# Moving part of a convolution's opening to GpSimd in a residual chain kernel

## The chip, the cores and the metric

The kernel runs on one core of one Trainium2 chip. The metric is the device time of one execution in microseconds; the median of three runs of the kernel before is 2248.76 us (2246.2 to 2252.79). The engines are named as the profile names them: PE is TensorE (matmuls), PEld its weight loads, DVE is VectorE, ACT is ScalarE, POOL is GpSimd and SP is SyncE, which issues most DMAs.

## The reference

The input is x of shape [32, 64, 1024] (batch, channel or row, position), and four lists of 32 integers. Four residual steps follow one another:

```python
x = x + conv(x, log_dt, C, log_A_real, A_imag, D, length)   # long convolution
x = x + einsum('bsi,boi->bso', x, w1[ids1])                  # adapter 1
x = x + einsum('bij,bkj->bik', x, w2[ids2])                  # adapter 2
x = x + lora_mlp(x, ids3)                                    # gated MLP with low-rank parts
```

Only the first matters for this change. Its kernel is a sum over 64 complex states for each of the 64 channels:

```python
dtA = (-exp(log_A_real) + 1j * A_imag) * exp(log_dt)[:, None]
Ct  = (C[..., 0] + 1j * C[..., 1]) * (exp(dtA) - 1) / A
K   = 2 * einsum('hn,hnl->hl', Ct, exp(dtA[:, :, None] * arange(1024))).real
y   = causal_convolution(x, K) + x * D[:, None]
```

and y is set to zero from each sequence's length on.

## The kernel before, in words

The convolution runs on chunks of 128 positions. For each pair of channels (32 pairs, held as 128 partitions = 2 channels x 64 states) the kernel needs powers of z = exp(dtA). It forms z to 37 chosen exponents (0, 32, 64, 96; 1 to 32; 128) as a magnitude (an exponential of the real part times the exponent) times a cosine and a sine of the phase times the exponent. From these few tables all 129 powers of a pair are made as products of two of them.

The pairs go through in groups of four, eight groups in all, and each group in two units of two pairs. The tables are made in two parts: part 0 holds the 8 pairs of groups 0 and 1, part 1 the 24 pairs of groups 2 to 7. A table row of part 0 has 8 x 37 = 296 columns, one of part 1 has 24 x 37 = 888.

For a unit, `products` (on ACT, 16 small activations, L1575) or `products_now` (on DVE, four tensor_tensor operations) write the products `m`; two DVE sums, kept in `adds`, turn them into the powers `zs`, and a POOL copy writes their first column (L1557). `powers_turned` transposes the powers on PE (L1624) and ACT copies them to `e` (L1637). `inputs` multiplies the input blocks by them on PE (L1655), and ACT copies the result to the states `xg` (L1663). `kernels` makes the convolution's first 128 taps (PE L1675, ACT L1692) and SP writes them to a scratch in DRAM, `kps`, whose rows begin with 128 zeros that POOL's queue wrote before; `load_taps` reads them back as a shifted matrix `hk`. `direct` applies the taps within a chunk (L1754). `scan` is the recurrence that carries the states from chunk to chunk: six steps of three dependent DVE operations. `carried` adds the states' part on PE (L1770), and `taken` masks the result and adds it to x on DVE.

The order of the work is written out by hand for DVE, ACT, POOL, SP and PE: each engine runs its instructions in the order in which the program emits them. `run(steps, events)` takes the steps of a recurrence one by one and inserts each event after the given number of steps; `spread` gives consecutive numbers. `opening` fills the pipeline before the first regular `period`: its units 0 to 2 come ahead of the first recurrence, its fourth unit (group 1, unit 1) between that recurrence's steps. The arguments of part 1 (`raised(1, ...)`, `fraction`) are made on DVE between the units, its exponential on ACT at L1877, its cosine and sine (`turned`) at L1338, L1339 and L1402, the products of magnitude and phase (`sizes`), the tables (`tables(1)`, `sz`) and the five small tables (`small_tables(1)`: `taps`, `turn`) between the recurrence's later steps. Helpers record most operations, so DVE's lines are mostly L1310 (`tt`), L1315 and L1317 (`ts`) and L1321 (`stt`), and the tiles tell them apart. Weights of the adapters are prefetched on SP's queue all along (`fetch`), into buffers that come free as the convolution ends.

The argument of part 1's exponential lies in `work[0]`, which is also the scratch of `tables`. The tile `opened` holds part 0's magnitude and, behind it, the zero row; the recurrence's scratch `t` takes the same buffer afterwards.

Of the kernel before, what the change touches and what calls it, by code (L numbers as in the profile page):

```python
# [19 lines left out]
P = 128  # L20
# [1215 lines left out]
def convolution(tc, cst, consts, xt, xf, ssm, eye, lens, x0, cd, ps_tile, fetch, places, rows_now, first):  # L1236
# [12 lines left out]
    with ExitStack() as ctx:  # L1249
# [53 lines left out]
        def small():  # L1303
            return space(NP)

        def col(i):
            return cst[:, i : i + 1]

        def tt(o, a, b, op):
            nc.vector.tensor_tensor(o, a, b, op)  # L1310
            return o

        def ts(o, a, c0, op0, c1=None, op1=None):
            if op1 is None:
                nc.vector.tensor_scalar(o, a, c0, None, op0)  # L1315
            else:
                nc.vector.tensor_scalar(o, a, c0, c1, op0, op1)  # L1317
            return o
# [12 lines left out]
        def fraction(v, k):  # L1331

            ts(k, v, MAGIC, ALU.add)
            stt(v, k, MAGIC, v, ALU.subtract, ALU.subtract)

        def cosine(o, r, k, scale=1.0):

            nc.scalar.activation(k, r, AF.Abs)  # L1338
            nc.scalar.activation(o, k, AF.Sin, scale=-scale, bias=col(CO_HALF))  # L1339

        def flipped(v, d):

# [27 lines left out]
        def by_part(pool, name, shape):  # L1370
# [5 lines left out]
        zts, szs = by_part(s1, "zt", [NL]), by_part(s1, "sz", [NA])  # L1376
        turns, tapss = by_part(g0, "turn", [2]), by_part(s1, "taps", [2, NA])
        rhos = [
            v[:, : (q1 - q0) * NL].rearrange("p (q l) -> p q l", l=NL)
            for v, (q0, q1) in zip((opened, work[0]), parts)  # L1380
        ]

        def of(tiles, q0, q1):
            i = int(q0 >= N0)
            return tiles[i][:, :, q0 - parts[i][0] : q1 - parts[i][0]]

        def raised(i, o, v):

            q0, q1 = parts[i]
            tt(  # L1390
                o,
                v[:, q0:q1].unsqueeze(2).to_broadcast([P, q1 - q0, NL]),
                cst[:, CO_LVAL : CO_LVAL + NL].unsqueeze(1).to_broadcast([P, q1 - q0, NL]),
                ALU.mult,
            )

        def turned(i, between=None):
            k, r = zts[i][:, 0], zts[i][:, 1]
            cosine(k, r, k, TURN)
            if between:  # L1400
                between()
            nc.scalar.activation(r, r, AF.Sin, scale=-TURN)  # L1402

        def sized(i):
# [3 lines left out]
        def tables(i):  # L1408


            q0, q1 = parts[i]
            n = q1 - q0
            t = work[0][:, : 4 * n * NA].rearrange("p (s j q a) -> p s j q a", s=2, j=2, a=NA)
            z = zts[i][:, :, :, :NA]
            s = [
                v[:, q0:q1].unsqueeze(1).unsqueeze(3).to_broadcast([P, 2, n, NA])
                for v in (s_re, s_im)
            ]
            tt(t[:, 0], z, s[0], ALU.mult)
            tt(t[:, 1], flipped(z, 1), s[1], ALU.mult)  # L1420
            for j, op in enumerate((ALU.subtract, ALU.add)):
                tt(szs[i][:, j], t[:, 0, j], t[:, 1, j], op)

        def small_tables(i):
            n = parts[i][1] - parts[i][0]

            def taps(j):
                side = cst[:, CO_SIDE + 2 * j : CO_SIDE + 2 * j + 2]
                tt(
                    tapss[i][:, j],  # L1430
                    szs[i][:, j].unsqueeze(2).to_broadcast([P, n, 2, NA]),
                    side.unsqueeze(1).unsqueeze(3).to_broadcast([P, n, 2, NA]),
                    ALU.mult,
                )

            def turn():
                z = [zts[i][:, j, :, NL - 1] for j in range(2)]
                nc.vector.tensor_copy(turns[i][:, 0], z[0].unsqueeze(2).to_broadcast([P, n, 2]))
                nc.vector.tensor_copy(turns[i][:, 1, :, 1], z[1])
                ts(turns[i][:, 1, :, 0], z[1], -1.0, ALU.mult)  # L1440

            return (lambda: taps(0)), (lambda: taps(1)), turn

# [17 lines left out]
        gp(pi, cre, aim, ALU.mult)  # L1461
        gp(v, cim, ea, ALU.mult)
        gp(pi, pi, v, ALU.add)
        t, em, ep, yh, u, sh, ch, w = (small() for _ in range(8))
        nc.scalar.activation(t, x, AF.Tanh, scale=0.5)
        nc.scalar.activation(rhos[0], rhos[0], AF.Exp)
        turns_off(y, u, (C1, C2, C3))
        ts(yh, y, 0.5, ALU.mult)
        ts(r, y, 1.0 / TWO_PI, ALU.mult)
        raised(0, zts[0][:, 1], r)  # L1470
        fraction(zts[0][:, 1], zts[0][:, 0])
        nc.scalar.activation(sh, yh, AF.Sin)
        cosine(ch, yh, w)
        turned(0)
        ts(em, t, -1.0, ALU.mult, 1.0, ALU.add)
        nc.vector.reciprocal(em, em)
        stt(em, t, 2.0, em, ALU.mult, ALU.mult)
# [35 lines left out]
        tt(rm, rm, m0, ALU.add)  # L1513
        stt(h4, acr, 2.0, rm, ALU.mult, ALU.add)
        nc.scalar.activation(m0, h4, AF.Sqrt)
        nc.vector.reciprocal(rm, m0)
        tt(rm, rm, h4, ALU.mult)
        tt(rm, rm, m0, ALU.add)
# [11 lines left out]
        tables(0)  # L1530

        kps = dram.tile([H, KROW], F32, tag="kp", name="kp")
        zero = opened[:H, N0 * NL : N0 * NL + P]
        nc.gpsimd.memset(zero, 0.0)
        nc.gpsimd.dma_start(kps[:, :P], zero)

        lnf = g0.tile([P, B], F32, tag="lnf", name="lnf")
        mask = g0.tile([P, NCK, KT, BC], F32, tag="mask", name="mask")
        maskf = mask.rearrange("p c k b -> p (c k b)")
        nc.gpsimd.tensor_copy(lnf, ln)  # L1540

        powers = {}

# [39 lines left out]
        def products_now(g, u, js=(0, 1), new=None):  # L1583
            m, q = new or new_powers(g, u)
            fs = []
            for j in js:
                z = of(zts, q + j, q + j + 1)[:, :, 0]
                s = of(szs, q + j, q + j + 1)[:, :, 0]
                for c in range(2):

                    def product(j=j, c=c, z=z, s=s):
                        tt(
                            m[:, c, j],
                            z[:, :, NA : NA + LQ].unsqueeze(2).to_broadcast([P, 2, NA, LQ]),
                            s[:, c].unsqueeze(1).unsqueeze(3).to_broadcast([P, 2, NA, LQ]),
                            ALU.mult,
                        )

                    fs.append(product)
            return fs  # L1600
# [16 lines left out]
        def powers_turned(g, u):  # L1617

            i_ = first_unit[g] + u
            zs = powers[i_]  # L1620
            ps = ps_tile(f"pt{i_}").rearrange("p (j i t) -> p j i t", j=2, i=2)
            for j in range(2):
                for i in range(2):
                    nc.tensor.matmul(  # L1624
                        ps[:, j, i],
                        zs[:, i, j, :P],
                        unit,
                        start=(i == 0 and j == 0),
                        stop=True,
                        is_transpose=True,  # L1630
                        skip_group_check=True,
                    )
# [226 lines left out]
        def opening():  # L1859


            warm(WARM)
            m0 = new_powers(0, 1)
            made(products(0, 1, (0,), m0))
            now(products_now(0, 0))
            added_now(0, 0)
            powers_turned(0, 0)()
            now(products_now(0, 1, (1,), m0))
            added_now(0, 1)
            powers_turned(0, 1)()  # L1870
            raised(1, rhos[1], x)
            now(small_tables(0))
            now(products_now(1, 0))
            added_now(1, 0)
            raised(1, zts[1][:, 1], r)
            fraction(zts[1][:, 1], zts[1][:, 0])
            nc.scalar.activation(rhos[1], rhos[1], AF.Exp)  # L1877
            inputs(0, 0)
            inputs(0, 1)
            kernels(0)  # L1880
            load_taps(0)
            fetch(MID)
            powers_turned(1, 0)()
            fourth = products_now(1, 1)
            sizes = [
                lambda j=j: tt(zts[1][:, j], zts[1][:, j], rhos[1], ALU.mult) for j in range(2)
            ]

            def second():
                turned(1, powers_turned(1, 1))  # L1890
                inputs(1, 0)
                inputs(1, 1)
                kernels(1)
                direct(0, 0)
                direct(0, 1)

            def third():
                tables(1)
                for u in range(2):
                    made(products(2, u))  # L1900

            run(
                scan(0),
                [
                    *spread(1, fourth),
                    *spread(5, adds.pop((1, 1))),
                    (7, second),
                    (8, masks),
                    *spread(9, sizes),
                    (10, third),  # L1910
                    *spread(12, small_tables(1)),
                ],
            )
            load_u(2)
            load_taps(1)
# [300 lines left out]
```

## Time and profile before

| | |
|---|---|
| median of three runs | 2248.76 us |
| the profiled execution | 2251.07 us, of which the span is 2249.4 us |
| granted TensorE clock, mean | 0.998 |
| busy: PE, PEld | 2198.9 us (98%), 1803.9 us (80%) |
| busy: DVE, ACT, POOL | 1370.9 us (61%), 424.1 us (19%), 207.5 us (9%) |
| DMA | 656.35 MB, mean 292 GB/s |
| convolution | from the start to about 143 us, where the adapters' matmuls (L315) begin to follow one another |

The page gives the busy time of each engine, the chain of work that ended last, and the costliest groups. As the shares are means over stages with different limits, a change in the opening is read from the timelines of the first 50 us: each line has the start, the time of one or more equal instructions, the engine, the line of the program, what is written from what, and, in brackets, an idle time before it and what ended it. Busy spans on POOL are rough.

### The profile page before, as it was taken

To read this page: it belongs to the slowest core of one execution; us is meant where nothing else is said; L and a number is where in the kernel's file an instruction comes from. 1 tells how busy PE (TensorE), PEld (TensorE's weight loads), DVE (VectorE), ACT (ScalarE), POOL (GpSimd) and SP (SyncE) were. 2 spreads that over 40 slices of the span, in tenths; PEclk is the share of its full clock that TensorE was granted. 3 is DMA by queue.
4 is the path that set the end of the run, shared out by engine and by line. 5 is a ranking of instruction groups with operands and counts; after the bars stand their busy time and mean duration, and the time that the engine had idled before them with its cause. 6 is when DMAs were issued, how large, how long until landed. Compare 5 with 4: busy or idle time off the path is not lost.

```text
span 2249.4 us, 53713 instructions
## 1 busy us (share of the span) xinstructions
PE 2198.9 (98%) x21488; PEld 1803.9 (80%) x21488; DVE 1370.9 (61%) x2995; ACT 424.1 (19%) x1042; POOL 207.5 (9%) x328
## 2 busy tenths in 40 slices
PE   7989999999999999999999999999999999999999
PEld 5755587777687897888688887789678988899998
DVE  8961277666367767466345667466336666576575
ACT  6800121111010112121012212022002212121220
POOL 1001021111012211000000111000000010100000
PEclk9999999999999999999999999999999999999999
DMA  8799998899979658799979839799979938385581
GB/s 312 252 316 401 386 359 306 316 363 356 344 294 354 241 174 303 290 366 358 351 266 367 298 128 343 263 337 358 364 281 354 337 116 282 111 291 189 203 278 63
DMA packets 204683, 656.35 MB, mean 292 GB/s; under 512 B 24066, under 2 KB 40834, under 8 KB 203922
## 3 DMA queue, kind: packets, MB, share of 16 engines
q1 hardware_dynamic: 173122, 565.84, 69.4%
q0 software_dynamic: 23392, 76.07, 9.2%
q10 hardware_dynamic: 7920, 11.01, 1.3%
q8 instruction: 169, 2.77, 0.5%
q14 instruction: 80, 0.66, 0.1%
HBM read 585.66 MB, written 67.17 MB: 290 GB/s over the span
## 4 chain that ended last, share of the span: by engine, by line
PE 79%; DMA 10%; DVE 6%; issue 4%; POOL 1%; ACT 1%; SPq 0%; POOLq 0%; DVEq 0%; ACTq 0%
PE pq L694 29%; PE po L1104 24%; PE pa L315 13%; DMA wa<-in_w 7%; PE pf L593 6%; PE pr L342 3%; PE pe L462 2%; DVE xg L1310 1%; PE pl_d L433 1%; DMA sums<-kept 1%; DVE t L1310 1%; DMA wr_first<-in_wr 1%; DVE tmp L1310 1%; PE pr_first L342 0%; ACT m L1575 0%
## 5 line engine op out<-in xcount | busy, mean ns | idle before, releaser
L315 PE MATMUL pa<-wa,x 128*32 128x256 f32 x7680 | 441.1, 380 | 16.7 <-DMA wa<-in_w 15.5
L694 PE MATMUL pq<-xd,wa 128*128 128x128 f32 x3360 | 414.9, 275 | 0.1
L315 PEld LDWEIGHTS pa<-wa,x 128*32 128x32 f32 x7680 | 238.4, 110 | 202.5 <-DMA wa<-in_w 42.1
L694 PEld LDWEIGHTS pq<-xd,wa 128*128 128x128 f32 x3360 | 394.6, 192 | 0.5 <-DMA wa<-sums 0.3
L694 PE MATMUL pq<-xd,wb 128*128 128x128 f32 x2520 | 323.6, 276 | 0.0
L694 PEld LDWEIGHTS pq<-xd,wb 128*128 128x128 f32 x2520 | 300.5, 192 | 3.6
L325 DVE STREAM_TRANSPOSE y<-pa 128x512 f32<-128x512 f32 x64 | 45.9, 717 | 287.9 <-PE pa L315 287.9
L1104 PE MATMUL po<-act,wd 128*128 128x256 f32 x640 | 168.6, 386 | 0.0
L1104 PE MATMUL po<-actd,wd 128*128 128x256 f32 x640 | 164.2, 379 | 0.0
L1104 PE MATMUL po<-actd,s 128*128 128x256 f32 x640 | 164.2, 379 | 0.0
L488 DVE TENSOR_TENSOR s<-wd 128x256 f32<-128x256 f32 x80 | 33.8, 423 | 176.5 <-PE po L1104 176.4
L1104 PEld LDWEIGHTS po<-act,wd 128*128 128x128 f32 x640 | 117.8, 190 | 29.3 <-issue 13.9
L593 PE MATMUL pf<-xd,wf 128*128 128x256 f32 x576 | 135.5, 381 | 0.0
L1104 PEld LDWEIGHTS po<-actd,s 128*128 128x128 f32 x640 | 121.6, 190 | 16.5
L1104 PEld LDWEIGHTS po<-actd,wd 128*128 128x128 f32 x640 | 121.6, 190 | 16.5
L1136 ACT COPY uo<-po 128x256 f32<-128x256 f32 x48 | 17.9, 373 | 620.1 <-PE po L1104 603.8
L361 POOL DMA_INDIRECT bgu<-in_bgu,rows x44 | 44.6, 1013 | 963.8 <-PE pe L462 798.4
L593 PEld LDWEIGHTS pf<-xd,wf 128*128 128x128 f32 x576 | 108.7, 190 | 15.5
L593 PE MATMUL pf<-xd,s 128*128 128x256 f32 x480 | 114.4, 381 | 1.0 <-DVE up L634 0.6
L718 ACT COPY u<-pq 128x256 f32<-128x256 f32 x120 | 41.5, 346 | 370.1 <-PE pq L694 303.2
L593 PEld LDWEIGHTS pf<-xd,s 128*128 128x128 f32 x480 | 90.3, 190 | 16.6 <-DVE up L634 2.7
L723 DVE TENSOR_TENSOR u<-u,u 128x256 f32<-128x256 f32 x120 | 46.6, 388 | 73.6 <-ACT u L720 73.6
(273 smaller groups left out, 2762.4 us busy)
## 6 DMA issues: line engine op xcount, KB each, us to landing
wa<-in_w SPq DMA_DIRECT2D x480, 512.0 KB
wa<-sums SPq DMA_DIRECT2D x210, 512.0 KB
wb<-parts SPq DMA_DIRECT2D x120, 384.0 KB
wd<-in_wd SPq DMA_DIRECT2D x80, 512.0 KB
wb<-in_wq SPq DMA_DIRECT2D x90, 384.0 KB
sums<-kept POOLq DMA_DIRECT2D x30, 1024.0 KB, 7.5
wf<-in_wu SPq DMA_DIRECT2D x20, 512.0 KB
uf<-in_xf SPq DMA_DIRECT2D x16, 512.0 KB
```

What stands on the lines that cost most here:

```text
L315: nc.tensor.matmul(acc[i * S : (i + 1) * S, s * 256 : (s + 1) * 256], xs[c][:, kt, lo + s * S : lo + (s + 1) * S], wt[:, i * 256 : (i + 1) ...
L325: nc.vector.transpose(y, acc)
L342: nc.tensor.matmul(ps[:, tokens], wt[:, kt, :], xs[c][:, kt, tokens], start=(kt == 0), stop=(kt == KT - 1),)
L361: nc.gpsimd.indirect_dma_start(out=t, out_offset=None, in_=table, in_offset=bass.IndirectOffsetOnAxis(ap=at_, axis=0),)
L462: nc.tensor.matmul(ps[:, at_ * 2 * H : (at_ + 1) * 2 * H], bt[pair(j), g], tms[table][pair(j)], start=(g == 0), stop=True, skip_group_chec ...
L488: nc.vector.tensor_add(s1, a21, a22)
L593: nc.tensor.matmul(ps, ws[j][:, kt, :], xb[j][:, kt, :], start=start and kt == 0, stop=kt == KH - 1, skip_group_check=True,)
L694: nc.tensor.matmul(ps[:, to * TQ : (to + 1) * TQ], w[i][:, k, :], xb[:, j, SLOT[i], k, :], start=start and k == 0 and to == 0, stop=k == K ...
L718: nc.scalar.copy(u, pa)
L723: nc.vector.tensor_add(u, v, u)
L1104: nc.tensor.matmul(pss[j], *term, start=(s0 == m0 and i == 0 and home[j] % 2 == 0), stop=(end and i == len(terms) - 1 and not late), skip_ ...
L1310: nc.vector.tensor_tensor(o, a, b, op)
```

## The change

Six things change in the opening.

- The argument of part 1's exponential (`raised(1, rhos[1], x)`, 888 columns) goes from DVE to POOL, right after POOL's nine small products; it is written behind the first 128 columns of `work[0]`, clear of the scratch of `tables(0)`.
- The phase argument of part 1 (888 columns) goes to POOL as well, as four operations: the product, MAGIC added, MAGIC subtracted, and the difference that is left. On DVE it had been a product and two operations.
- Part 1's exponential on ACT goes from between the units to right behind the second square root.
- The zero row (memset, DMA) and the cast of the lengths go from right after those products on POOL's queue to behind the copies of the first two units.
- The fourth unit with its transposes, the magnitude (Abs), cosine and sine of part 1, the second group's inputs and kernels and the first group's direct products are emitted ahead of the first recurrence; the magnitude stands ahead of the third unit. Between the steps there remain the masks, the sizes and the tables.
- The five small tables of part 1 go to POOL, after `tables(1)`.

```diff
-            v[:, : (q1 - q0) * NL].rearrange("p (q l) -> p q l", l=NL)
-            for v, (q0, q1) in zip((opened, work[0]), parts)
+            v[:, at_ : at_ + (q1 - q0) * NL].rearrange("p (q l) -> p q l", l=NL)
+            for v, at_, (q0, q1) in zip((opened, work[0]), (0, 4 * N0 * NA), parts)
...
         gp(pi, pi, v, ALU.add)
+        raised(1, rhos[1], x, nc.gpsimd)
...
         ts(r, y, 1.0 / TWO_PI, ALU.mult)
+        k1, r1 = zts[1][:, 0], zts[1][:, 1]
+        raised(1, r1, r, nc.gpsimd)
+        nc.gpsimd.tensor_scalar(k1, r1, MAGIC, None, ALU.add)
+        nc.gpsimd.tensor_scalar(k1, k1, MAGIC, None, ALU.subtract)
+        gp(r1, k1, r1, ALU.subtract)
         raised(0, zts[0][:, 1], r)
...
         nc.scalar.activation(m0, h4, AF.Sqrt)
+        nc.scalar.activation(rhos[1], rhos[1], AF.Exp)
...
             powers_turned(0, 1)()
-            raised(1, rhos[1], x)
+            zeros()
+            second = turned(1)
+            next(second)
             now(small_tables(0))
             now(products_now(1, 0))
             added_now(1, 0)
-            raised(1, zts[1][:, 1], r)
-            fraction(zts[1][:, 1], zts[1][:, 0])
-            nc.scalar.activation(rhos[1], rhos[1], AF.Exp)
             inputs(0, 0)
             inputs(0, 1)
             kernels(0)
             load_taps(0)
             fetch(MID)
             powers_turned(1, 0)()
-            fourth = products_now(1, 1)
+            now(products_now(1, 1))
+            added_now(1, 1)
+            next(second, None)
+            powers_turned(1, 1)()
+            inputs(1, 0)
+            inputs(1, 1)
+            kernels(1)
+            direct(0, 0)
+            direct(0, 1)
...
             def third():
                 tables(1)
+                now(small_tables(1, nc.gpsimd))
                 for u in range(2):
                     made(products(2, u))
 
             run(
                 scan(0),
                 [
-                    *spread(1, fourth),
-                    *spread(5, adds.pop((1, 1))),
-                    (7, second),
-                    (8, masks),
+                    (7, masks),
                     *spread(9, sizes),
-                    (10, third),
-                    *spread(12, small_tables(1)),
+                    (11, third),
                 ],
             )
```

`turned` now yields after its magnitude, so that the cosine and the sine can be emitted later; `zeros` is a function that holds the memset, the DMA and the cast; `raised` and `small_tables` take the engine as an argument.

More of the change, by code (lines that the diff above doesn't have):

```diff
@@ L1334, in fraction, with cosine @@
             stt(v, k, MAGIC, v, ALU.subtract, ALU.subtract)
-        def cosine(o, r, k, scale=1.0):
+        def cosine(o, r, k):
             nc.scalar.activation(k, r, AF.Abs)
-            nc.scalar.activation(o, k, AF.Sin, scale=-scale, bias=col(CO_HALF))
+            nc.scalar.activation(o, k, AF.Sin, scale=-1.0, bias=col(CO_HALF))
         def flipped(v, d):
@@ L1385, in of, with raised @@
             return tiles[i][:, :, q0 - parts[i][0] : q1 - parts[i][0]]
-        def raised(i, o, v):
+        def raised(i, o, v, engine=nc.vector):
             q0, q1 = parts[i]
-            tt(
+            engine.tensor_tensor(
                 o,
@@ L1395, in raised, with turned @@
             )
-        def turned(i, between=None):
+        def turned(i):
             k, r = zts[i][:, 0], zts[i][:, 1]
-            cosine(k, r, k, TURN)
-            if between:
-                between()
+            nc.scalar.activation(k, r, AF.Abs)
+            yield
+            nc.scalar.activation(k, k, AF.Sin, scale=-TURN, bias=col(CO_HALF))
             nc.scalar.activation(r, r, AF.Sin, scale=-TURN)
@@ L1422, in tables, with small_tables @@
                 tt(szs[i][:, j], t[:, 0, j], t[:, 1, j], op)
-        def small_tables(i):
+        def small_tables(i, engine=nc.vector):
             n = parts[i][1] - parts[i][0]
@@ L1428, in taps @@
                 side = cst[:, CO_SIDE + 2 * j : CO_SIDE + 2 * j + 2]
-                tt(
+                engine.tensor_tensor(
                     tapss[i][:, j],
@@ L1437, in turn @@
                 z = [zts[i][:, j, :, NL - 1] for j in range(2)]
-                nc.vector.tensor_copy(turns[i][:, 0], z[0].unsqueeze(2).to_broadcast([P, n, 2]))
-                nc.vector.tensor_copy(turns[i][:, 1, :, 1], z[1])
-                ts(turns[i][:, 1, :, 0], z[1], -1.0, ALU.mult)
+                engine.tensor_copy(turns[i][:, 0], z[0].unsqueeze(2).to_broadcast([P, n, 2]))
+                engine.tensor_copy(turns[i][:, 1, :, 1], z[1])
+                engine.tensor_scalar(turns[i][:, 1, :, 0], z[1], -1.0, None, ALU.mult)
             return (lambda: taps(0)), (lambda: taps(1)), turn
@@ L1473, in convolution @@
         cosine(ch, yh, w)
-        turned(0)
+        for _ in turned(0):
+            pass
         ts(em, t, -1.0, ALU.mult, 1.0, ALU.add)
@@ L1532, in convolution @@
         kps = dram.tile([H, KROW], F32, tag="kp", name="kp")
-        zero = opened[:H, N0 * NL : N0 * NL + P]
-        nc.gpsimd.memset(zero, 0.0)
-        nc.gpsimd.dma_start(kps[:, :P], zero)
         lnf = g0.tile([P, B], F32, tag="lnf", name="lnf")
@@ L1539, in convolution, with zeros @@
         maskf = mask.rearrange("p c k b -> p (c k b)")
-        nc.gpsimd.tensor_copy(lnf, ln)
+        def zeros():
+            zero = opened[:H, N0 * NL : N0 * NL + P]
+            nc.gpsimd.memset(zero, 0.0)
+            nc.gpsimd.dma_start(kps[:, :P], zero)
+            nc.gpsimd.tensor_copy(lnf, ln)
         powers = {}
@@ L1887, in opening @@
             ]
[L1889 to L1895, printed above, removed]
             def third():
                 tables(1)
+                now(small_tables(1, nc.gpsimd))
                 for u in range(2):
```

## The prediction

> **What bounds the kernel now.** I read the page's busy shares first, then the chain of work that ended last in order of time, then the stretches of ten microseconds over the first 200 us, then the timelines of VectorE (DVE), ScalarE (ACT) and GpSimd (POOL) over the opening. TensorE is busy for 98% of the whole span, but the edit sits in the first 45 us, and there the stretches read like this (busy us and instruction counts of each engine, granted clock, DMA share, GB/s):
>
> ```profile
> 20.00:30.00 10.00, 6.90 (x66) 4.46 (x64) 9.76 (x26) 7.92 (x21) 1.35 (x4) 1.00 0.99 396
> 30.00:40.00 10.00, 5.71 (x28) 3.54 (x30) 9.90 (x24) 5.82 (x8) 0.00 (x0) 0.67 0.65 224
> 40.00:50.00 10.00, 9.38 (x82) 7.32 (x78) 9.35 (x25) 9.34 (x37) 1.12 (x4) 0.99 0.82 279
> 120.00:130.00 10.00, 8.50 (x66) 6.86 (x65) 9.62 (x26) 2.04 (x5) 0.00 (x0) 1.00 0.99 345
> 160.00:180.00 20.00, 17.39 (x304) 8.76 (x296) 2.81 (x4) 0.00 (x0) 8.81 (x16) 1.00 1.02 386
> ```
>
> DVE (third number) is the bound from 3 us to the end of the convolution: 9.4 to 9.9 of 10, while POOL is nearly empty. DVE's waits for others up to 143 us are 3.3 us for the first load, 1.6 us for ACT's products in three pieces, 1.0 us for TensorE and 0.4 us for a root. Does a microsecond saved here reach the end? The chain says what follows:
>
> ```profile
> 142.40 0.61 DVE x L1310
> 143.05 16.22 PE pa L315 x296
> 160.86 12.16 DMA wa<-in_w
> 173.14 12.40 DMA wa<-in_w
> ```
>
> The adapters start with DVE's last sum, and soon wait for weights. That stream keeps the DMA at 1.01 to 1.03 from 140 to 260 us, and its start is tied to the convolution: the last eight prefetches are issued at 135.53, when the direct products end (131.70 + 3.69), and the rotating loads at 143.75, when matmuls free buffers. From 30 to 140 us the DMA has slack (shares of 0.50 to 0.65 in three stretches). So I carry a shift of the convolution's end one to one to the end of the span.
>
> **What leaves DVE.** DVE's timeline (start, duration):
>
> ```profile
> 23.64 1.08 DVE L1310 TENSOR_TENSOR work<-work,cst 128x888 f32<-128x888 f32 x1
> 27.27 1.08 DVE L1310 TENSOR_TENSOR zt<-work,cst 128x888 f32<-128x888 f32 x1
> 28.38 0.62 DVE L1315 TENSOR_SCALAR zt<-zt 128x888 f32<-128x888 f32 x1
> 29.04 1.08 DVE L1321 SCALAR_TENSOR_TENSOR zt<-zt 128x888 f32<-128x888 f32 x1
> 30.04 0.69 DVE L1310 TENSOR_TENSOR t<-xg,turn 128x512 f32<-128x512 f32 x1
> 43.04 0.69 DVE L1310 TENSOR_TENSOR t<-xg,turn 128x512 f32<-128x512 f32 x1
> 43.76 0.88 DVE L1310 TENSOR_TENSOR xg<-xg,t 128x256 f32<-128x256 f32 x2
> 44.75 0.69 DVE L1310 TENSOR_TENSOR t<-xg,turn 128x512 f32<-128x512 f32 x1
> 45.85 0.42 DVE L1310 TENSOR_TENSOR zs<-m 128x256 f32<-128x256 f32 x1 [0.41 <-ACT m L1575]
> ```
>
> By start-to-start times the decay argument is worth 1.00 us (23.64 to 24.64), the phase argument with its fraction 2.77 (27.27 to 30.04), the five small tables 3 x 0.27 = 0.81: 4.58 us leave DVE. But the fourth unit (four products, two sums, 2.13 us by the third unit's 25.14 to 27.27) used to sit between the dependent steps of the first recurrence, and the tables too. A bare step takes 1.71 us (43.04 to 44.75); step two with three fillers of 0.34 took 2.28 (32.32 to 34.60), so 1.26 without them: 0.45 us of latency per bare step. Steps one, two and five become bare.
>
> The new DVE schedule, laid out from these rows: second unit done at 23.64; small tables 0.50, third unit 2.13, fourth unit 2.13: recurrence from 28.40. Two bare steps 3.42; step three with the mask 1.73; the sizes 1.00 and 1.11, step four's parts 0.60 + 0.34 + 0.45, the second part's tables 1.01; two bare steps 3.42. The next period starts at 41.5 instead of 44.75: 3.3 us earlier.
>
> **What could be late next.** ACT: the exponential with its table load (25.05 to 27.28) goes to behind the second root (16.52), where ACT idles 3.44 us before 19.96 and needs 1.28 + 0.94 = 2.22; if that cover fails, the excess falls on the eight products at 19.96. Then the magnitude ends at 26.0, the four state copies follow TensorE's products (ending 27.5) to 28.0, in time for 28.40; the table load and two sines (1.28 + 1.03 + 0.94, after the third unit's turned copy at 29.4) end at 32.7, and the sizes need them at 33.6 and 35.2. State copies of the second group then follow to about 36, the kernel row to 37, and the 16 products of the third group, gated by the tables, run from 37.5 to 41.4 (3.85 us), before the sum that waited 0.41 us at 45.85. So that wait goes too: 3.7 us in all. The zero row's memset, descriptor (0.76 us) and cast move on POOL's queue from 10.11 to about 22; the zero row shares a buffer with the recurrence's scratch, so the first step now waits for that DMA, and so does the first tap load (31.98 before). Some 5 us remain for it to land; if they don't suffice, each missing microsecond counts in full. SP's order of issues stays as it was.
>
> **What POOL costs.** No row shows an 888-column operation on POOL. Its memsets of 128 and 512 columns take 0.196 and 0.518 us: 0.84 ns a column, so 0.83 us for 888 if nothing but one stream counts; that is the lower end, 4.2 us for five. The upper end scales a 32-column row with its 0.24 us spacing by columns: 6.7 us each, 33 us. I take 0.83 for the two one-input operations and twice the stream, 1.58, for the three two-input ones: 6.4 us, POOL done near 17. I lean to the memset because most of a 32-column row is fixed cost. The Trainium skill (GPSIMD Engine Reference, Elementwise side-by-side) gives 4497 ns for 2048 fp32 columns of a two-input sum; my estimate from it is 1.95 us for 888, and the five would make some 7.5.
>
> **The shared read path**, the decisive unknown:
>
> ```profile
> 7.38 0.55 POOL L1456 TENSOR_TENSOR work<-par 128x32 f32<-128x32 f32 x1
> 7.39 0.45 DVE L1310 TENSOR_TENSOR opened<-work,cst 128x296 f32<-128x296 f32 x1
> 8.49 0.27 POOL L1459 TENSOR_TENSOR work<-par 128x32 f32<-128x32 f32 x1
> 49.52 2.40 POOL L1557 COPY zs<-sz 128x4 f32<-128x4 f32 x1 [2.10 <-PE py L1770]
> 51.79 0.68 DVE L1310 TENSOR_TENSOR tmp<-py,mask 128x512 f32<-128x512 f32 x1
> ```
>
> POOL's 32-column operation takes twice its usual time exactly when DVE reads two SBUF operands for 0.45 us. The copy of four columns, 0.19 us elsewhere, lasts 2.40 us and ends when DVE turns from such operations to one that reads PSUM and one SBUF operand (51.79). So DVE shuts POOL out. Whether a long POOL operation shuts DVE out, this trace cannot show: its POOL operations are too short. Bounds: nothing, to POOL's whole streaming, 6.4 us; a gain is excluded, as contention takes no work away. From 10.2 to 20 us DVE runs a serial chain of 32-column operations of about 0.2 us, most with two SBUF operands; POOL finds a gap after each and then streams. If exclusion works both ways, DVE gets about one operation in for each POOL operation: 6.4 - 5 x 0.2 = 5.4 us of delay. I take that end, because the only rows that show the two engines meeting show one shut out, and 0.5 us more for the small tables beside the bare steps (two of 192 columns, 0.41 each by the same slope, and three short ones). Nothing hides this; the chain feeds the first table at 19.96, and all later work.
>
> The Trainium skill (SBUF — State Buffer, Who interferes with whom) speaks against the change: a DVE instruction with two SBUF inputs and a GpSimd one that reads SBUF exclude each other, and whichever comes second "fully blocks" until the first finishes. The rows above agree for DVE first; for POOL first no run here shows it. By that rule and the other page's 7.5 us, the delay would be near 6.5; with ports that don't meet, nothing.
>
> **The sum.** -3.7 + 5.4 + 0.5 = +2.2 us. The profiled execution took 2251.07 us (span 2249.4 and 1.7 around it), 2.3 above the median of the runs shown (2248.76); on the median's scale: 2251.0.
>
> **Rivals.** (1) *No exclusion of DVE by POOL*: -3.7, 2245.1. For it: DVE's three-operand steps beside POOL between 8.2 and 8.9 us come every 0.225 us, no slower than the 0.25 us of the 64-column steps before POOL begins; against it, POOL streamed little there. (2) *POOL's queue is late* (slower): in its order the copies of the first column of the first unit stand behind the five operations, and TensorE's first transpose at 22.0 needs them; ACT's magnitude stands ahead of the state copies and needs the fifth. It decides when five operations take more than 22.0 - 10.2 = 11.8 us, 2.4 each; at 4 us each the transposes come 8.2 us late, which less 3.7 gives +4.5, and with some of the exclusion some +8: 2257. For it: the lower ends are linear guesses and three patterns broadcast; against it, the memset's slope would have to be three times off. (3) *More than it says*: TensorE's clock fell to 0.67 at 30 to 40 us after an idle 5.5 us; a kept clock would shorten the state products (5.52 us there, 3.25 at full clock) by 2.3 us. But DVE is the bound there, so this helps only if the waits for ACT's products go with it: at most the 1.2 us left of them, and with rival 1 and smaller bubbles some -7: 2242.
>
> **Chances.** Forecast 0.52 (2248 to 2254), rival 1 0.30 (2243.5 to 2247), rival 2 0.12, rival 3 0.06. The range 2243 to 2256 leaves out rival 3 and most of rival 2. About 0.3% (6.7 us) is what a measurement of this kernel can tell from no change: forecast and rival 1 lie within it, so same 0.81, slower 0.12, faster 0.07.
>
> **What would show it.** Exclusion: the first table's products start on DVE near 25.5 us instead of 19.96, with DVE operations of 1 to 2 us among the 32-column ones after 10 us. Rival 1: they start at 20 and the next period near 41.5. Rival 2: the first transpose waits for POOL. Wrong altogether: a first recurrence waiting for the zero row's DMA, or a convolution end whose shift is not met at 300 us.

## The result, and the profile after

The changed kernel takes 2251.24 us (median of 16 runs, 2248.33 to 2258.55) beside 2248.15 us of the kernel before on the same chips. The ratio is 1.0021 with a 95% interval of 1.0012 to 1.0030: some 4.7 us (2.7 to 6.7) slower, less than the 0.3% bound of the forecast. A second comparison gave 1.0017 (1.0007 to 1.0027). The profiled execution took 2250.81 us, with a span of 2249.1 us.

The stretches of the changed kernel, in the columns of before:

```profile
20.00:30.00 10.00, 3.22 (x14) 1.79 (x12) 9.10 (x37) 5.14 (x13) 3.54 (x8) 0.67 0.98 392
30.00:40.00 10.00, 8.36 (x75) 5.59 (x74) 7.89 (x20) 7.56 (x13) 0.00 (x0) 0.82 0.03 10
40.00:50.00 10.00, 7.16 (x62) 5.77 (x64) 9.62 (x20) 8.22 (x31) 3.40 (x7) 1.00 0.96 349
160.00:180.00 20.00, 17.32 (x284) 9.36 (x280) 3.41 (x5) 0.00 (x0) 7.97 (x15) 0.91 1.02 373
```

Two things are new. PE has 3.22 us of work from 20 to 30 us where it had 6.90, and its granted clock is 0.67 there and 0.82 in the next stretch (1.00 and 0.67 before). And DVE, once at 9.90 from 30 to 40 us, is busy for 7.89 us there, so idle for 2 us. From 160 us on the weights bound the kernel again. The chain shows the later start of the adapters:

```profile
144.85 0.61 DVE x L1310
145.50 13.63 PE pa L315 x248
160.19 9.74 DMA wa<-in_w
```

POOL's five argument operations, and beside them what happened to DVE (start, duration; both timelines of the changed kernel):

```profile
10.14 1.99 POOL L1390 TENSOR_TENSOR work<-work,cst 128x888 f32<-128x888 f32 x1
12.10 1.70 POOL L1390 TENSOR_TENSOR zt<-work,cst 128x888 f32<-128x888 f32 x1
13.89 2.47 POOL L1473 TENSOR_SCALAR zt<-zt 128x888 f32<-128x888 f32 x1
16.44 2.45 POOL L1474 TENSOR_SCALAR zt<-zt 128x888 f32<-128x888 f32 x1
18.97 2.07 POOL L1475 TENSOR_TENSOR zt<-zt 128x888 f32<-128x888 f32 x1
```

```profile
10.49 1.68 DVE L1317 TENSOR_SCALAR work<-work 128x32 f32<-128x32 f32 x1
12.20 0.35 DVE L1483 RECIPROCAL work<-work 128x32 f32<-128x32 f32 x1
12.59 1.25 DVE L1321 SCALAR_TENSOR_TENSOR work<-work 128x32 f32<-128x32 f32 x1
14.42 0.47 DVE L1321 SCALAR_TENSOR_TENSOR work<-work 128x32 f32<-128x32 f32 x1
16.63 0.83 DVE L1310 TENSOR_TENSOR work<-work 128x64 f32<-128x64 f32 x1
19.01 2.08 DVE L1310 TENSOR_TENSOR work<-work 128x32 f32<-128x32 f32 x1
25.30 1.43 DVE L1310 TENSOR_TENSOR m<-zt,sz 128x256 f32<-128x256 f32 x4
35.67 0.69 DVE L1310 TENSOR_TENSOR t<-xg,turn 128x512 f32<-128x512 f32 x1 [1.83 <-issue]
```

Read the two side by side. A DVE operation on 32 columns takes some 0.2 us otherwise (0.17 to 0.19 us next to these rows); here one lasts 1.68 us and ends at 12.17, just after POOL's first product does (12.13); one lasts 2.08 us and ends at 21.09, after POOL's last (21.04). The three long ones fall on POOL's three two-operand products. During POOL's one-operand operations, which last longest, DVE loses only some 0.3 and 0.6 us. The reciprocal keeps its 0.35 us. So the first table's products start at 25.30 us instead of 19.96: 5.34 us late. The last line is a new wait of 1.83 us, and PE's timeline shows where it comes from:

```profile
27.34 1.15 PE L1634 MATMUL pt<-unit,zs 128*128 128x128 f32 x4 [6.37 <-DVE zs L1310]
29.96 5.04 PE L1665 MATMUL pv<-uf,e 128*64 128x224 f32 x32
```

PE sat idle for 6.37 us, because the first powers were late, and the 32 state products behind it took 5.04 us instead of the 3.25 us of before. Here is their row in PE's timeline of before, and the last of ACT's copies of the states in the changed kernel's:

```profile
24.26 3.25 PE L1655 MATMUL pv<-uf,e 128*64 128x224 f32 x32
35.05 0.53 ACT L1673 COPY xg<-pv 128x448 f32<-128x448 f32 x1 [0.23 <-PE pv L1665]
```

The copies follow the products, and the first recurrence needs the copies: the last one ends at 35.58 us, and the recurrence starts at 35.67. The profile itself names nothing that DVE waited for here ("issue"); the experiments below do.

### The profile page after: what moved, and what is told of

Same layout as the page of the kernel before. It is cut to its first block, busy times and chain, and to the rows that moved or that the text cites. A ratio compares the mean times of both kernels' runs of the same rounds, so it can differ in the third digit from the quotient of the medians.

```text
span 2249.1 us, 53710 instructions
## 1 busy us (share of the span) xinstructions
PE 2197.9 (98%) x21488; PEld 1806.3 (80%) x21488; DVE 1372.0 (61%) x2986; ACT 424.5 (19%) x1042; POOL 220.9 (10%) x338
## 4 chain that ended last, share of the span: by engine, by line
PE 82%; DMA 9%; DVE 5%; issue 3%; POOL 0%; ACT 0%; SPq 0%; POOLq 0%; DVEq 0%; ACTq 0%
PE pq L694 29%; PE po L1104 24%; PE pa L315 14%; PE pf L593 7%; DMA wa<-in_w 5%; PE pr L342 3%; DMA wa<-sums 2%; PE pe L462 2%; DVE xg L1310 1%; PE pl_d L433 1%; DVE t L1310 1%; DVE tmp L1310 1%; DMA wr_first<-in_wr 1%; DMA sums<-kept 1%; PE pr_first L342 0%
## 5 line engine op out<-in xcount | busy, mean ns | idle before, releaser
L325 DVE STREAM_TRANSPOSE y<-pa 128x512 f32<-128x512 f32 x64 | 45.8, 716 | 283.1 <-PE pa L315 283.1
L718 ACT COPY u<-pq 128x256 f32<-128x256 f32 x120 | 41.5, 346 | 371.5 <-PE pq L694 304.9
```

Source lines behind the costliest of these rows:

```text
L325: nc.vector.transpose(y, acc)
L718: nc.scalar.copy(u, pa)
```

## The experiments

The theory was that a long GpSimd operation shuts DVE out of the path that both use, and that this, less what DVE no longer does, is the whole change. Rivals: no such exclusion, with the new order to blame; a wait for the zero row's DMA instead of a clock drop; and a gain or loss in the opening that does not reach the end. This table collects the marks (us from the span's start, from DVE's and PE's timelines); "16th sum" is the start of the 16th of the 64 adapter transposes (L325). Medians stand beside the kernel before on the same chip.

| kernel | first products | first recurrence | next period | adapters | 16th sum | median / before | ratio (95%) |
|---|---|---|---|---|---|---|---|
| before | 19.96 | 30.04 | 44.75 | 143.05 | 283.4 | | |
| before_again | 19.97 | 30.05 | 44.76 | 143.00 | 283.6 | 2249.27 / 2248.40 | 1.0006 (0.9995 to 1.0017) |
| changed | 25.30 | 35.67 | 48.87 | 145.50 | 285.5 | 2251.24 / 2248.15 | 1.0021 (1.0012 to 1.0030) |
| after_again | 25.23 | 35.83 | 49.03 | 145.62 | 286.4 | 2251.86 / 2248.40 | 1.0017 (1.0007 to 1.0027) |
| args_dve | 19.89 | 32.10 | 45.28 | 142.72 | 282.5 | 2247.72 / 2248.54 | 0.9997 (0.9986 to 1.0009) |
| args_only | 25.26 | 35.44 | 50.16 | 146.65 | 285.9 | 2250.38 / 2248.54 | 1.0009 (0.9999 to 1.0020) |
| after_warm | 25.32 | 33.78 | 46.97 | 144.40 | 285.3 | 2254.23 / 2248.54 | 1.0028 (1.0019 to 1.0037) |
| args_short | 19.90 | 28.38 | 41.57 | 139.09 | 278.6 | 2246.53 / 2248.45 | 0.9997 (0.9988 to 1.0006) |
| args_short_again | 20.00 | 28.48 | 41.67 | 138.19 | 278.5 | 2246.51 / 2248.40 | 0.9996 (0.9985 to 1.0008) |
| tables_only | 19.95 | 30.03 | 44.74 | 141.27 | 281.7 | 2247.77 / 2248.45 | 1.0000 (0.9991 to 1.0010) |
| exp_act | 19.96 | 29.05 | 43.76 | 141.91 | 281.7 | 2249.42 / 2248.45 | 1.0009 (0.9999 to 1.0019) |
| exp_act_fill | 19.90 | 28.98 | 43.70 | 140.88 | 282.7 | 2249.39 / 2248.45 | 1.0002 (0.9992 to 1.0012) |
| exp_tables | 20.01 | 29.09 | 43.80 | 141.79 | 283.2 | 2247.30 / 2248.40 | 0.9993 (0.9982 to 1.0004) |

**ports: the disputed cost by itself.** A kernel of its own, run once, in phases; most have one chain on DVE and a few operations on GpSimd:

```python
for _ in range(2):
    G.tensor_tensor(g3, gb[0], gb[1], ALU.mult)      # or tensor_scalar, or memset; 888 columns
for _ in range(24):
    V.scalar_tensor_tensor(v, v, 1.0, w[:, :32], ALU.mult, ALU.mult)   # or another kind
```

> A small kernel that leaves the whole computation out and only measures the two engines side by side: VectorE chains of 24 dependent operations of 128x32 (two SBUF operands, one operand, reciprocal, one PSUM operand) alone and beside two 888-column GpSimd operations, and 20 independent 128x256 products beside the same. Mutual exclusion: the two-operand chain alone takes about 24 x 0.22 = 5.4 us; beside two products on GpSimd of some 1.9 us each it takes 3 to 4 us more, with single VectorE operations stretched to 1.5 us and more; the reciprocal chain and the chain with a PSUM operand are not stretched; memsets on GpSimd cost the chain nothing. Beside the long independent VectorE products it is GpSimd that is held, until they end (some 6.8 us). Exclusion of GpSimd by VectorE alone (rival 1 of the prediction): every VectorE chain keeps 0.22 us a step.

DVE's chains in order: alone (va), beside two GpSimd products (vc), beside two GpSimd tensor_scalar (vd); then a tensor_scalar chain (ve), a reciprocal chain (vf) and one with a PSUM operand (vh), each beside two GpSimd products; then the first chain beside memsets (vi); last, 20 long independent products beside two GpSimd products (vj):

```profile
2.99 5.37 DVE L121 SCALAR_TENSOR_TENSOR va<-va,ones 128x32 f32<-128x32 f32 x24
23.96 8.20 DVE L142 SCALAR_TENSOR_TENSOR vc<-vc,ones 128x32 f32<-128x32 f32 x24
32.70 6.77 DVE L150 SCALAR_TENSOR_TENSOR vd<-vd,ones 128x32 f32<-128x32 f32 x24
40.02 7.97 DVE L159 TENSOR_SCALAR ve<-ve 128x32 f32<-128x32 f32 x24
48.54 6.17 DVE L168 RECIPROCAL vf<-vf 128x32 f32<-128x32 f32 x16
55.25 5.27 DVE L177 TENSOR_TENSOR vh<-vh,pone 128x32 f32<-128x32 f32 x24
61.06 5.40 DVE L185 SCALAR_TENSOR_TENSOR vi<-vi,ones 128x32 f32<-128x32 f32 x24
67.26 9.80 DVE L194 TENSOR_TENSOR vj<-ones 128x256 f32<-128x256 f32 x20
```

And GpSimd's operations in the same kernel, first alone (gb), then beside the chains vc and vd:

```profile
8.94 3.47 POOL L127 TENSOR_TENSOR gb<-ones 128x888 f32<-128x888 f32 x2
16.75 4.94 POOL L131 TENSOR_SCALAR gb<-gb 128x888 f32<-128x888 f32 x2
21.75 1.73 POOL L133 MEMSET gb<- 128x888 f32 x2
24.08 3.53 POOL L140 TENSOR_TENSOR gc<-ones 128x888 f32<-128x888 f32 x2
32.83 4.94 POOL L148 TENSOR_SCALAR gd<-big 128x888 f32<-128x888 f32 x2
```

The chain of two-operand steps loses 2.83 us beside two products, 1.42 for each of some 1.76 us; beside two tensor_scalar 1.40, 0.70 for each of 2.47 us, so there DVE is held for a part of the time only. A chain of DVE's own tensor_scalar is shut out as well (0.33 us a step; its steps stand 0.22 apart in the kernel before). The reciprocal keeps 0.39 us a step, as in the kernel before; the chain with a PSUM operand 0.22; and memsets cost nothing. GpSimd is not slowed by these chains: 3.53 beside 3.47. One part of what was expected failed: beside long independent DVE products (128x256, 20 of them) GpSimd was not held until they ended. It got its turn, and the 20 took 9.80 us instead of the expected 6.8. So it is DVE that pays here too. When GpSimd waits instead, as its copy of four columns did for 2.40 us in the kernel before, these runs do not settle. The exclusion works both ways, and rival 1 of the prediction falls.

**args_dve: the arguments back on DVE.** The five POOL operations go; the rest of the change stays.

```diff
-        raised(1, rhos[1], x, nc.gpsimd)
...
-        raised(1, r1, r, nc.gpsimd)
...
             zeros()
+            raised(1, rhos[1], x)
...
             added_now(1, 0)
+            raised(1, zts[1][:, 1], r)
+            fraction(zts[1][:, 1], zts[1][:, 0])
+            nc.scalar.activation(rhos[1], rhos[1], AF.Exp)
```

> The changed kernel with the two arguments of the second part back on VectorE at their places of before (and the exponential behind them); the fourth unit stays ahead of the first recurrence, the small tables stay on GpSimd. If exclusion by GpSimd's long operations is the price: the first table's products start at 20.0 us again (25.3 in the changed kernel), no clock drop on TensorE ahead of the first transpose, the next period starts near 45.3 (48.87; before 44.75) and the adapters' matmuls near 142 us (145.5; before 143.05), since VectorE's waits for ACT's products (1.6 us before) stay away. If the new order itself is what costs (bare recurrence steps), the adapters start at 145 us again.

The products start at 19.89 us, the next period at 45.28 (expected 45.3), the adapters at 142.72 (expected 142). The order by itself (with the small tables on POOL) costs 0.5 us up to the next period; from there to the adapters 0.9 us come back, 0.6 of them because DVE's waits for ACT's products shrink from 1.6 to 1.0 us. The time is that of before. The new order is not to blame.

**args_only: the arguments on POOL, the old order.**

```diff
+        raised(1, rhos[1], x, nc.gpsimd)
+        raised(1, r1, r, nc.gpsimd)
+        nc.gpsimd.tensor_scalar(k1, r1, MAGIC, None, ALU.add)
...
-            raised(1, rhos[1], x)
-            raised(1, zts[1][:, 1], r)
-            fraction(zts[1][:, 1], zts[1][:, 0])
```

> The kernel before with only the arguments on GpSimd, the exponential behind the roots and the zero row behind the first copies; the fourth unit stays between the recurrence's steps and the small tables on VectorE. Exclusion: first products at 25.3 us as in the changed kernel. With the first recurrence emitted ahead of the fourth unit, its first step meets the state copies at 35.6 us with nothing to do before it, so VectorE waits some 4 us there and the adapters start at 147 to 148.5 us, later than in the changed kernel (145.5). If the price comes from the new order and not from GpSimd, the adapters start ahead of 143 us.

DVE's timeline of this kernel:

```profile
35.44 0.69 DVE L1310 TENSOR_TENSOR t<-xg,turn 128x512 f32<-128x512 f32 x1 [3.78 <-ACT xg L1672]
```

Products at 25.26 us, a wait of 3.78 us for the state copies, both as expected, and the adapters at 146.65 us, a little under the 147 to 148.5 expected. In the changed kernel the fourth unit stands in that gap, and about half of it is covered. The wait is named here: ACT's copies.

**after_warm: is it the clock, or the zero row?** `WARM = 20` becomes `WARM = 30`.

> The changed kernel with 30 instead of 20 rounds of TensorE's idle matmuls at the start, to fill the gap from 20.96 to 27.34 us after which the state products took 5.04 us instead of 3.25. If the 1.83 us wait ahead of the first recurrence comes from TensorE at a lower granted clock (state products late, so state copies late): state products back to 3.3 us, wait near 0.1, adapters' start 1.7 us earlier, near 143.8 us. If that wait is for the zero row's DMA, which shares the buffer of the recurrence's scratch: wait and adapters' start as in the changed kernel, 1.8 and 145.5 us.

PE's and DVE's timelines of this kernel:

```profile
29.62 3.25 PE L1665 MATMUL pv<-uf,e 128*64 128x224 f32 x32
134.34 3.69 PE L1764 MATMUL py<-uf,hk 128*128 128x256 f32 x16 [2.53 <-DMA hk<-kp]
```

```profile
33.78 0.68 DVE L1310 TENSOR_TENSOR t<-xg,turn 128x512 f32<-128x512 f32 x1
```

The state products are back at 3.25 us, the granted clock from 20 to 40 us is 1.00, and the wait is gone, though POOL issues the zero row's DMA at the same time as in the changed kernel (26.57 and 26.55 us): it was the clock, not the DMA. The recurrence starts at 33.78 us, where the prediction's 28.40 and 5.4 us put it. The next period comes 1.9 us earlier. But the adapters start only 1.1 us earlier: at 49.77 us DVE meets a new wait of 0.77 us for TensorE, whose granted clock was 0.75 from 45 to 50 us. The 16th sum comes hardly earlier (285.3 and 285.5): the last direct products wait for their taps' DMA until 134.34 us (134.16 in the changed kernel), and the last prefetches are issued when they end. That it was this issue, and not the adapters' start, that set the stream of weights here fits, but is not shown: the 16th sum moves by 0.9 us between two profiles of the changed kernel, and exp_tables speaks against it (last section). Why this kernel's runs are slower still (1.0028, an interval that overlaps the changed kernel's) was not found.

**args_short: the change without long streams.** POOL's five operations work on 37 columns; the other arguments are zeros from memsets at the start, so most of that computation is left out.

```diff
-        raised(1, r1, r, nc.gpsimd)
-        nc.gpsimd.tensor_scalar(k1, r1, MAGIC, None, ALU.add)
+        r1_, k1_ = r1[:, :1], k1[:, :1]
+        raised(1, r1, r, nc.gpsimd, 1)
+        nc.gpsimd.tensor_scalar(k1_, r1_, MAGIC, None, ALU.add)
...
```

> The changed kernel, but GpSimd makes the arguments of one pair of the second part only (37 columns instead of 888); the other 23 pairs keep zeros that GpSimd writes at the very start, so this part of the computation is left out. Same order, same instructions, no long stream. Exclusion: the first table's products start at 20.2 us (25.3 in the changed kernel), the first recurrence near 28.7 without a wait for the state copies (35.7), the next period near 42, the adapters' matmuls near 139 us (145.5; before 143.05), and the gain of some 4 us should still stand at 300 us, where the first MLP weights are kept (299.6 before, 301.6 changed), and in the time: 2244 to 2245 us beside 2248.5. If something other than the streams delays VectorE (order, the table load ahead of the exponential, POOL's queue), the products stay near 25 us. If the stage that waits for weights gives the gain back, it is gone at 300 us.

DVE's timeline:

```profile
19.90 1.43 DVE L1310 TENSOR_TENSOR m<-zt,sz 128x256 f32<-128x256 f32 x4
28.38 0.69 DVE L1310 TENSOR_TENSOR t<-xg,turn 128x512 f32<-128x512 f32 x1
41.57 0.69 DVE L1310 TENSOR_TENSOR t<-xg,turn 128x512 f32<-128x512 f32 x1
```

This is the change with its price taken away, and within 0.1 us the prediction's layout: recurrence at 28.38 (28.40 laid out), next period at 41.57 (41.5). The adapters start 4.0 us earlier than before, the 16th sum 4.8 us, and at 300 us the gain still stands (the first MLP weights are kept from 294.71 us, from 299.48 before). But the time does not follow in full: 1.9 us by the medians, 0.7 by the ratio, with an interval that ends at 2.7.

**tables_only, exp_act, exp_act_fill: parts that free DVE otherwise.** The first is the kernel before with `small_tables(1, nc.gpsimd)`. The second leaves GpSimd alone and makes the magnitudes on ACT:

```diff
+        def magnitudes(i0, i1):
+            for i in range(i0, i1):
+                nc.scalar.activation(
+                    rhos[1][:, i],
+                    cst[:, CO_LVAL : CO_LVAL + NL],
+                    AF.Exp,
+                    scale=x[:, N0 + i : N0 + i + 1],
+                )
...
-            raised(1, rhos[1], x)
-            nc.scalar.activation(rhos[1], rhos[1], AF.Exp)
```

The third adds eight idle matmuls between the third and the fourth unit's transposes.

> The kernel before with only the five small tables of the second part on GpSimd. They take 0.81 us of VectorE's spacing between recurrence steps there. Exclusion: two short streams beside bare recurrence steps stretch two VectorE operations by 0.2 to 0.25 us each, and the steps lose three fillers, so the next period starts 0 to 0.4 us earlier than 44.75 and the time does not move (within 1 us). Without exclusion: 0.4 to 0.8 us earlier.

> The kernel before with another way to free VectorE, without GpSimd: the second part's magnitudes are made on ACT, pair by pair, as exponentials of the exponents scaled by each pair's decay (24 activations of 37 columns), 12 behind the second root, 12 behind the third unit's turned copy; the 888-column product on VectorE and the 888-column exponential go. ACT's own ports mean no stretch of VectorE: first products at 20.0 us as before, the first recurrence 1.0 us earlier (29.0), the adapters 1.0 us earlier (142.0). If offloading as such pays nothing here, since ACT's products are late by 1.6 us in all, the adapters stay at 143.

> The same as exp_act and, besides, 8 idle matmuls of 256 columns on TensorE between the third unit's and the fourth unit's transposes, where it sat idle for 5.5 us before and then ran the second group's state products at a lower granted clock (5.52 us instead of 3.25). If the clock drop is what makes ACT's products late, the state products take 3.3 us, VectorE's waits for ACT's products (1.6 us before) shrink below 0.8 us, and the adapters start at 140.5 to 141.5 us. If those waits come from ACT's own work, they stay, and the adapters start at 142 as in exp_act.

The tables alone move the next period by 0.01 us: what leaves DVE (0.81 us) comes back as stretched steps and lost fillers. The adapters nevertheless start 1.8 us earlier. By the traces that is no merit of the tables: in this profile PE's clock came back sooner, so ACT's products began 1.0 us earlier (40.86 against 41.88 us) and DVE's 1.6 us of waits for them went. The second group's state products, first in the kernel before, then in tables_only:

```profile
35.57 5.52 PE L1655 MATMUL pv<-uf,e 128*64 128x224 f32 x32
35.56 4.51 PE L1655 MATMUL pv<-uf,e 128*64 128x224 f32 x32
```

The same tables added to exp_act (exp_tables) move its adapters by 0.1 us only (141.79 against 141.91). exp_act gives 0.99 us at the recurrence and 1.14 at the adapters, as expected. With the fill the state products take 3.25 us and the waits shrink to 0.2 us; the adapters start at 140.88 us, but the last direct products run until 135.4 us as in the kernel before (130.02, 5.38 us long), so the 16th sum gains 0.6 us only. None of the three moves the time beyond its interval.

**before_again, after_again, args_short_again, exp_tables: how far can this be trusted, and is there a better kernel?** Three kernels once more, and exp_act with tables_only's edit.

> The kernel before once more, unchanged: how far one profile's marks and one comparison's ratio can be trusted. If the convolution's end is fixed by the program, the adapters start at 143.0 us again (within 0.3), while the marks after 300 us move by 1 to 3 us from profile to profile, and the ratio's interval holds 1. If the first profile was an unusual one, the start moves by more than 1 us, and the gains and losses of the other kernels have to be read against both.

> The changed kernel once more: adapters' start at 145.5 us (within 0.3), first products at 25.3, VectorE's wait ahead of the first recurrence 1.8 us; time 2 to 5 us over the kernel before. If the loss at the end is something else than the opening's 2.5 us, the marks at 283 us and the time don't go together.

> The kernel with 37-column argument streams once more (most arguments left at zero): adapters' start at 139.1 us. If a shift of the convolution's end reaches the end of the span, the time is 4 us under the kernel before (ratio 0.998); if the stages after 300 us that wait for weights take it back, the ratio stays within 0.999 to 1.0005 as in its first comparison.

> The kernel before with the magnitudes made on ACT pair by pair and the small tables on GpSimd: the two parts that freed VectorE without a long stream. First recurrence at 29.0 us, next period at 43.5 to 43.8, adapters' start at 140 to 141 us (143.05 before). If such shifts reach the end, 2 to 3 us under the kernel before; if not, no difference that can be told.

The opening repeats: the adapters start within 0.05 us in the kernel before and 0.12 in the changed one (0.9 in args_short). What follows does not: the start of the 29th adapter sum, 618.0 us in the first profile of before, was 615.4 in the second. The kernel before against itself gave 1.0006 (0.9995 to 1.0017). The changed kernel is slower in both comparisons, and args_short in neither faster beyond its interval. exp_tables is the fastest by its ratio, 0.9993, and not to be told from the kernel before; its adapters started at 141.79 us, not at 140 to 141. No version here beats it clearly.

## Why the prediction was right, and where it was not

The forecast was 2251.0 us with exclusion as the likeliest case; 2251.24 us was measured, and the case held. That the two totals lie so close is in part luck: the shift was forecast as +2.2 us from a median of 2248.76, and it was +3.1 by the medians (from 2248.15) and +4.7 by the ratio, whose interval (2.7 to 6.7) leaves 2.2 out; the second comparison (+3.8, 1.6 to 6.1) does not. By its steps:

- *What leaves DVE and the new layout*: right. Without the streams, DVE reaches the recurrence at 28.38 us and the next period 3.2 us ahead of before (laid out: 3.3). The 0.5 us booked besides for the small tables came as 0.36: the fifth step took 2.08 us in args_short (37.77 to 39.85), the sixth 1.72. It hardly shows, because the first two bare steps took 1.64 us each where 1.71 was laid out.
- *The shared path*: right in kind and, by luck, in size: 5.4 us predicted, 5.34 measured at the first products. The prediction let DVE stand still for all of POOL's streaming, less one operation for each of the five (6.4 - 5 x 0.2). POOL's one-operand operations were put at 0.83 us from the memsets' slope and took 2.45 us, and the products, put at 1.58 us, took 1.70 to 2.07 us. So POOL was busy until 21.04 us, not 17, for 10.9 us in all, and the same sum would have come to some 9.9. What made up for it is that the one-operand operations held DVE for some 0.3 and 0.6 us only: the DVE operation beside each ended some 1.0 us after POOL's had begun (14.89 against 13.89, 17.46 against 16.44). The products held single DVE operations for 1.5, 1.1 and 1.9 us. The rule of the Trainium skill (SBUF — State Buffer, Who interferes with whom) put the delay near 6.5 us, by the prediction's estimate. With GpSimd first, which the trace of before could not show, the runs now agree with its list of what contends: two-operand steps and tensor_scalar did, steps with one PSUM operand did not. They differ on the hold "for the whole instruction": DVE lost 0.70 us beside a tensor_scalar of 2.47 us.
- *What could be late next*: this step failed. "The four state copies follow TensorE's products (ending 27.5) to 28.0, in time for 28.40" moved the copies and the recurrence alike with the delay, and left out that PE would be idle for 6.4 us ahead of them and run slower afterwards: 1.83 us of new wait, which after_warm takes away. The clock was named only as a possible gain, in rival 3.
- *ACT's products*: 0.41 us was booked; in fact the waits fell from 1.6 to 0.3 us, as two later ones went too. This made up for most of the clock's price.
- The terms at the next period: -3.2 from the new order and what left DVE (args_short), +5.5 from the streams and +1.8 of wait (35.67 against 28.38, args_short's recurrence, is 7.3) make +4.1 us (48.87 against 44.75); less 1.3 of waits, +2.8; the adapters' start shows +2.45. DVE's busy time from the next period to its last sum is 0.26 us shorter (93.07 against 93.33), which makes up the rest; why was not traced.
- *One to one to the end*: not shown. The opening's +2.5 us became +2.1 and +3.0 at the 16th sum and, by the ratios, +4.7 and +3.8 at the end (intervals from 1.6 to 6.7); args_short's -4.0 and -4.9 became -0.7 and -0.9 (the two intervals reach from -3.4 to +1.8). So the four microseconds that args_short saves in the opening do not come out in full. The marks of single profiles, where args_short keeps 6.4 and 4.9 us to the end, say otherwise, but they move by 2 to 3 us from one profile to the next. Whether a later wait for weights takes the gain back is open.
- *Rival 2*, POOL's queue late, did not come: POOL was done at 21.04 us, before the first copy's 25.43. Against the 11.8 us at which it was to decide, the five operations took 10.9; the two one-operand ones took the threefold of the memset's slope that the prediction held to be unlikely. Rival 3 did not come either.

## What to carry to other kernels

Work moved to GpSimd cost VectorE nothing here where VectorE meanwhile ran reciprocals or operations with one PSUM operand, or where GpSimd's work was a memset. A chain of short two-operand steps, or of tensor_scalar, lost some 1.4 us for each 888-column product. Before moving work, lay the row of the engine that is to take it beside the chain of the engine that gives it. And when a chain is delayed ahead of TensorE, price TensorE's idle time too: 6.4 us without matmuls made the next 32 slower by 1.8 us.

## What the runs showed of the hardware that was not expected

- A one-operand fp32 tensor_scalar of 888 columns takes longer on GpSimd (2.47 us) than a two-operand product (1.74 us with broadcast operands), and a memset 0.87 us; yet beside short two-operand steps it holds DVE for only half as long as the product (0.70 against 1.42 us each).
- How soon the granted clock returns after idleness is not fixed by the program: the same 32 state products after the same 5.5 us of idleness took 5.52 and 5.47 us in two profiles of the kernel before, and 4.51 in tables_only, which ran the same work up to there. What decides it was not found.
- When the stream of weights starts is open. In the two kernels whose last direct products did not end earlier, the adapters moved up by 1.1 and 2.2 us (after_warm, exp_act_fill) and the 16th sum by 0.1 and 0.6 us only, as if the issue of the last prefetches behind those products set it. But in exp_tables both the prefetches (134.23 against 135.53 us) and the adapters came 1.3 us earlier, and the 16th sum 0.2 us.
